# Attention and gated feed-forward in one interleaved kernel: the first sequence's long attention steps turned by VectorE blocks and DMA, as in the other sequences

## The chip, the cores and the metric

The kernel runs on one core of one Trainium2 chip. The time is device microseconds (us) of one execution; a kernel's time is the median of its runs.

## What is computed

Four sequences of 512 rows with 512 columns go through a layer norm, and then through two branches. One is causal attention with 16 heads of 32 columns (normed and rotated queries and keys). The other is a gated feed-forward of 1408 hidden columns whose weights come as integers with a scale. The result is the input plus the product of the branches:

```python
def reference(x, ...):
    xn = _layernorm(x, axis=-1)
    q, k, v = split(xn @ w_qkv)              # 16 heads of 32
    q, k = rotate(rmsnorm(q, q_gamma)), rotate(rmsnorm(k, k_gamma))
    attn = softmax(where(causal, q @ k.T / sqrt(32), -1e30))
    s = (attn @ v) @ w_out
    W = lambda wq, scale: (wq - 128.0) * scale[:, None]
    h = silu(xn @ W(wq_gate, s_gate).T) * (xn @ W(wq_up, s_up).T)
    g = silu(h @ W(wq_down, s_down).T)
    return x + s * g
```

## The kernel before, in words

**Parts.** The work is cut into 16 parts `(b, g)`: sequence `b` of 0 to 3, and group `g` of 0 to 3, which is four heads (one each on 32 of TensorE's rows) and a chunk of the 11 blocks of hidden columns (2 blocks in `g = 0`, 3 in the others). A part has two windows. In the *hidden window* (`hidden_window`) TensorE computes gate and up of the chunk's blocks (`hidden`, L577, 16 matmuls of 512 columns for each block), ScalarE and VectorE form the gated product (L588 to L596), and `fresh.turn` (L416) transposes this part's queries and keys into `qT` and `kT`. In the *attention window* four steps `t` of 128 query rows follow, with 128, 256, 384 and 512 keys: scores on TensorE (L444), the masked minimum on VectorE (L465), the exponential on ScalarE (L475), the transposed probabilities times `v` on TensorE (`values`, L531). Between them stand the chunk's down projection (`contract`, L606, with its addition on VectorE, L617 or L619) and the projection of queries, keys and values for the next part (`product`, L368, and `rotate`, L383 to L406, on ScalarE, VectorE and GpSimd). The order of all of this is written out by hand: every engine takes its instructions in the order in which the code issues them.

**Two ways to turn probabilities.** `Step.turn` (L491, L125, L127) has TensorE transpose 128x128 squares into PSUM, and ScalarE or VectorE copy them to SBUF. `Step.blocks` (L508) has VectorE transpose 32x32 squares within SBUF, one instruction for each head, and `Step.spread` (L522) moves the blocks to their partitions by four DMAs of SyncE's queue (192 KB each for 384 keys, 256 KB each for 512).

**Two orders.** Parts of sequence 0 use `attention_window` (L723): steps 0 to 2 are turned by TensorE there, the four products of the projection are spread over the window, and step 3 is turned by TensorE in the next hidden window (`drain`, L679), at whose end its `values` stand (L721). Parts of sequences 1 to 3 but the very last use `placed_window` (L788): steps 0 and 1 are turned by TensorE with ScalarE's copies, step 2 by `blocks` and `spread`; then come the four products one after the other, then the values of steps 0 to 2, and step 3's scores. Step 3 is turned by `blocks` and `spread` in the next hidden window, and its `values` stand in the next attention window. `swapped(b)` (L419), which is `b > 0`, chooses. The very last part has `last_window`.

**Weights.** The feed-forward's integer weights are prepared in sequence 0 beside the parts, up to the third hidden window, by `weights()` (L278), which is called after each block of a hidden window and after each product of an attention window. One call handles two pieces: it finishes two that were turned at least two calls ago (`finish_weights`, L265, VectorE), starts the loads of two (`load_weights`, L247, SyncE's queue, 256 KB each), and turns two that were loaded in an earlier call (`turn_weights`: a cast on ScalarE, L256, then a DMA transpose on SyncE's queue, L258). A load's room comes free at a finish, so the loads of a call wait for that call's finishes. SyncE's queue issues in order: what waits there holds up all behind it. After the third hidden window `find_wide` (L293 to L297) reduces a flag on VectorE and TensorE.

Of the kernel before, what the change touches and what calls it, by code (L numbers as in the profile page):

```python
# [51 lines left out]
def interleaved(  # L52
# [225 lines left out]
    def weights(n=2):  # L278

        now[0] += 1  # L280
        for _ in range(n):
            if turning and now[0] - turning[0][0] >= 2:
                finish_weights()
        load_weights(n)
        for _ in range(n):
            if loaded and now[0] - loaded[0][0] >= 1:
                turn_weights()
# [11 lines left out]
    units = [(b, g) for b in range(B) for g in range(NC)]  # L299
# [116 lines left out]
                    nc.tensor.transpose(tp[:, ts(t, P)], self.qk[t][:, ts(i, P)], ident)  # L416
                copy(i == 0, dst, tp)

    def swapped(b):  # L419

        return b > 0


    class Step:
        def __init__(self, b, g, t, v, sums, pv):
            self.b, self.g, self.t, self.v, self.sums, self.pv = b, g, t, v, sums, pv
            self.keys = (t + 1) * P
            self.id = f"{b}_{g}_{t}"

            self.per = min(HPG, N // self.keys)  # L430
            self.pieces, self.probs, self.turned = [], [], []
            self.before = None
            self.placed = swapped(b) and (b, g) != units[-1]
            if self.placed:
                self.first, self.way = (8, 9, 0, 0)[t], (None, None, 8, 4)[t]

# [236 lines left out]
    def hidden_window(b, g, last, fresh, result, norm, beside):  # L673

        placed = last is not None and last.placed

        def drain(i):  # L679
            if last is not None and not placed:  # L680
                last.turn(i, scalar=False)
                last.turn(i + 1, scalar=True)

        def turned(*tiles):
            if norm is not None:
                for t in tiles:
                    norm.turn(t)

        fills = [
            lambda: drain(0),  # L690
            lambda: drain(2),
            lambda: (last.spread_sums() if last is not None else None, fresh.turn()),
            lambda: turned(0, 1),
            lambda: turned(2),
            lambda: turned(3),
        ]
        for i, f in enumerate(chunks[g]):
            bank = hidden(b, f, 0, other=placed and i == 0)
            sil = gate(b, f, bank)
            if placed and i == 0:  # L700
                last.blocks(0, 1, 2)
            if fills:
                fills.pop(0)()
            bank = hidden(b, f, 1, other=placed and norm is None and f == chunks[g][-1])
            gated(sil, f, bank, h[:, i])
            if placed and i == 0:
                last.blocks(3)
                last.spread()
            if fills:
                fills.pop(0)()  # L710
            if result is not None:
                result.gate(2 * i)
                result.gate(2 * i + 1)
            for e in beside[i]:
                e()
            if b == 0:
                weights()
        if last is not None:
            last.turn_sums()
            if not placed:  # L720
                last.values()  # L721

    def attention_window(b, g, last, s, fresh, norm):  # L723

        def halves(*tiles):
            if norm is not None:
                for t in tiles:  # L730
                    norm.cut(t)

        def project(t):
            fresh.product(t)

        def rotate(t):
            fresh.rotate(t)

        def beside(t):
            weights()  # L740

        s[0].scores()
        s[1].scores(s[0].whole, s[0].keys)
        s[0].probabilities(0, 1, 2, 3)
        add = contract(b, g, 0)
        s[1].probabilities(0)
        add()
        s[1].probabilities(1, 2, 3)
        if last is not None:
            last.divide()  # L750
        add = contract(b, g, 1, other=True)
        halves(0, 1)
        s[0].turn(0, scalar=False)
        project(0)
        add()
        rotate(0)
        beside(0)
        add = contract(b, g, 2)
        s[0].values()
        s[2].scores()  # L760
        add()
        s[2].probabilities(0, 1, 2, 3)
        s[1].turn(0, scalar=True)
        s[1].turn(1, scalar=False)
        project(1)
        rotate(1)
        halves(2, 3)
        beside(1)
        add = contract(b, g, 3)
        s[1].values()  # L770
        s[3].scores()
        add()
        s[3].probabilities(0, 1)
        s[2].turn(0, scalar=True)
        s[3].probabilities(2)
        s[2].turn(1, scalar=False)
        s[3].probabilities(3)
        project(2)
        s[2].turn(2, scalar=True)
        s[2].turn(3, scalar=False)  # L780
        rotate(2)
        beside(2)
        project(3)
        s[2].values()
        rotate(3)
        beside(3)

    def placed_window(b, g, last, s, fresh, norm, result):  # L788

        def halves(engine, *tiles):
            if norm is not None:
                for t in tiles:
                    norm.cut(t, engine)

        def beside(t):
            if result is not None:
                result.project(t)
                result.finish(t)  # L800

        def load(*tiles):
            if result is not None:
                for t in tiles:
                    result.load(t)

        load(0)
        s[0].scores()
        s[1].scores(s[0].whole, s[0].keys)
        s[0].probabilities(0, 1, 2, 3)  # L810
        add = contract(b, g, 0)
        s[1].probabilities(0, 1, 2, 3)
        add()
        add = contract(b, g, 1, other=True)
        if last.placed:
            last.values()
        s[2].scores()
        add()
        s[2].probabilities(0, 1)
        add = contract(b, g, 2)  # L820
        s[0].turn(0, scalar=True)
        s[2].probabilities(2)
        s[1].turn(0, scalar=True)
        s[2].probabilities(3)
        s[1].turn(1, scalar=True)
        s[2].blocks(0, 1, 2, 3)
        s[2].spread()
        load(1, 2)
        add()
        last.divide()  # L830
        halves(nc.gpsimd, 0, 1)
        for t in range(NT):
            fresh.product(t, other=t == NT - 1)
            fresh.rotate(t)
            if t == 1:
                halves(nc.vector, 2, 3)
            beside(t)
            if t == 1:
                load(3)
        for t in range(3):  # L840
            s[t].values()
        s[3].scores()
        s[3].probabilities(0, 1, 2, 3)
        contract(b, g, 3)()
# [103 lines left out]
    fresh, last, norm, done = prologue(), None, None, None  # L948
    for u, (b, g) in enumerate(units):
        result = Result(b - 1) if g == 0 and b else None  # L950
        done = result or done
        beside = [[], [], []]
        if g == NC - 2 and b + 1 < B:
            for t in range(NT):
                load_x(b + 1, t)
            norm = Norm(b + 1)
            beside[1] += [lambda t=t: norm.stats(t) for t in (0, 1)]
            beside[2] += [lambda t=t: norm.stats(t) for t in (2, 3)]
            beside[2].append(lambda: norm.roots(slice(0, NT)))
        if g == NC - 1 and b + 1 < B:  # L960
            for i, tiles in enumerate(((0, 1), (2, 3))):
                beside[i] += [lambda t=t: norm.apply(t) for t in tiles]
        due = norm if g == NC - 1 and b + 1 < B else None
        hidden_window(b, g, last, fresh, result, due, beside)
        if g == 1 and b:
            for t in range(NT):
                done.store(t)
        if (b, g) == (0, NC - 1):
            nc.sync.dma_start(wout, w_out.rearrange("(c p) m -> p c m", p=P))
        if (b, g) == (0, NC - 2):  # L970
            find_wide()
        s = steps(b, g, fresh.v)
        if u + 1 == len(units):
            break
        fresh = Projection(*units[u + 1])
        if swapped(b):
            placed_window(b, g, last, s, fresh, due, result)
        else:
            attention_window(b, g, last, s, fresh, due)
        last = s[3]  # L980
    result = Result(B - 1)
    for t in range(NT):
# [474 lines left out]
```

## Time and profile before

| | us |
|---|---|
| median of 3 runs (lowest, highest) | 694.18 (692.93, 695.31) |
| the profiled execution's own time | 694.41 |
| its span, first to last instruction | 692.6 |
| TensorE busy in the span | 646.3 (93%) |
| VectorE busy | 442.3 (64%) |
| ScalarE busy | 364.6 (53%) |
| GpSimd busy | 321.3 (46%) |
| mean granted TensorE clock | 0.987 |

A part is told here from its first score matmul to the next part's. Those of sequence 0 start at 41.62, 83.76, 126.37 and 167.35 us from the span's start, those of sequence 1 at 203.19, 252.13, 288.69 and 327.15, and sequence 2 begins at 363.66. The page's lines give, for a group of instructions, the source line, the engine, the operation, the tiles written and read, the shape and the count; then busy time and the mean of one; then the idle time of the engine just before them, and what ended it. A row of the timeline gives start, duration, engine, line and operation, and in brackets the engine's idle time ahead of it with the instruction that ended it.

### The profile page before, as it was taken

Reading aid. Unit: us, or ns where it says so; the run is one execution under the profiler, and the core shown is the slowest. Engines: PE = TensorE matmul, PEld = TensorE weight load, DVE = VectorE, ACT = ScalarE, POOL = GpSimd, SP = SyncE. Lnnn points to the kernel's source line nnn. Section 1 sums busy time; section 2 is a strip of 40 time slices with the busy share of each in tenths; the row PEclk is TensorE's granted clock in tenths of the full one; section 3 lists DMA queues with packets and bytes.
Section 4 is the critical chain, followed back from the end, with each engine's and each line's share of the span. In section 5 each row is a group of like instructions: output and inputs, shape, how many; then the busy total and the mean of one; then the engine's idle time right before and its main releaser. Section 6 shows DMA issues by size and latency. Waiting matters only on the chain.

```text
span 692.6 us, 11843 instructions
## 1 busy us (share of the span) xinstructions
PE 646.3 (93%) x4078; PEld 435.0 (63%) x4078; DVE 442.3 (64%) x1206; ACT 364.6 (53%) x931; POOL 321.3 (46%) x371
## 2 busy tenths in 40 slices
PE   4969999999998999999989999999997999999895
PEld 3645857667674576768665576767665566666652
DVE  3548676755665466867777367788686466757563
ACT  3466666556563264646746055465747146464550
POOL 4905434452754625545462732627281641727322
PEclk9989999999999999999999999999999999999998
DMA  7673744100003044222222134312123304222401
GB/s 245 170 180 102 183 109 103 62 1 1 1 17 92 1 121 108 62 46 63 46 58 55 56 79 113 95 39 38 38 45 77 92 2 121 46 62 47 122 1 66
DMA packets 47408, 51.36 MB, mean 74 GB/s; under 512 B 21206, under 2 KB 31212, under 8 KB 47340
## 3 DMA queue, kind: packets, MB, share of 16 engines
q1 hardware_dynamic: 46380, 50.10, 28.6%
q8 instruction: 34, 0.56, 0.3%
q10 hardware_dynamic: 960, 0.43, 0.2%
q14 instruction: 34, 0.28, 0.1%
HBM read 21.80 MB, written 4.19 MB: 38 GB/s over the span
## 4 chain that ended last, share of the span: by engine, by line
PE 80%; DVE 7%; ACT 6%; DMA 3%; issue 2%; POOL 1%; SPq 1%; DVEq 0%; ACTq 0%
PE qkv L368 24%; PE h L577 21%; PE dn L606 9%; PE so L649 8%; PE pv L531 5%; PE sc L444 5%; PE pt L491 4%; ACT arena L475 2%; PE qkt L416 2%; DVE sil L594 1%; DMA oT<-in_L_ffn_wq_up 1%; POOL h L596 1%; PE xnt L344 1%; ACT arena L125 1%; DVE arena L508 1%
## 5 line engine op out<-in xcount | busy, mean ns | idle before, releaser
L475 ACT ACTIVATE arena<-arena,least 128x128 f32<-128x128 f32 (+3 forms) x256 | 141.2, 553 | 70.8 <-DVE least L465 70.7
L368 PE MATMUL qkv<-wqkv,xnT 128*128 128x384 f32 x512 | 173.3, 491 | 2.3 <-DVE least L465 2.3
L368 PEld LDWEIGHTS qkv<-wqkv,xnT 128*128 128x128 f32 x512 | 96.0, 192 | 66.7 <-issue 5.1
L465 DVE CUSTOM_DVE_ANT_0 arena<-sc,mask 128x128 f32<-128x128 f32 (+3 forms) x256 | 109.9, 487 | 33.8 <-PE sc L444 33.6
L404 POOL TENSOR_TENSOR qk<-qk,qs 128x256 f32<-128x256 f32 x64 | 46.7, 730 | 169.6 <-DVE qs L399 169.6
L596 POOL TENSOR_TENSOR h<-sil,h 128x512 fp32r<-128x512 f32 x44 | 58.3, 1324 | 120.8 <-ACT h L595 120.8
L315 POOL TENSOR_TENSOR ss<-ss,minus_half 128x8 f32<-128x8 f32 x64 | 106.8, 1669 | 5.3
L606 PE MATMUL dn<-wdT,h 128*128 128x512 f32 x352 | 100.3, 421 | 4.9 <-POOL h L596 2.9
L508 DVE STREAM_TRANSPOSE arena<-arena 128x384 f32<-128x384 f32 (+1 forms) x88 | 81.2, 968 | 15.9 <-ACT arena L475 11.1
L606 PEld LDWEIGHTS dn<-wdT,h 128*128 128x128 f32 x352 | 63.2, 191 | 42.5 <-issue 18.4
L383 ACT ACTIVATE squares<-qkv 128x256 f32<-128x256 f32 x64 | 24.7, 385 | 122.2 <-PE qkv L368 103.9
L594 DVE SCALAR_TENSOR_TENSOR sil<-h,scales,sil 128x512 f32<-128x512 f32 x44 | 32.6, 741 | 65.4 <-PE h L577 53.6
L396 DVE TENSOR_TENSOR qk<-qkv,tab 128x256 f32<-128x256 f32 x64 | 27.0, 421 | 72.6 <-ACT v L384 72.1
L595 ACT CAST h<-sil 128x512 fp32r<-128x512 f32 x44 | 27.3, 621 | 76.8 <-DVE sil L594 76.8
L649 PE MATMUL so<-wout,oT 128*128 128x512 f32 x128 | 58.1, 593 | 0.0
L444 PE MATMUL sc<-kT,qT 32*128 32x512 f32 (+3 forms) x512 | 50.8, 478 | 5.9 <-ACT qT L125 5.9
L577 PE MATMUL h<-xh,wuT 128*128 128x512 f32 x176 | 51.0, 412 | 5.2 <-DVE kT L127 5.2
L491 PE MATMUL pt<-ident,arena 128*128 128x128 f32 x332 | 46.7, 276 | 6.5 <-ACT arena L125 6.4
L491 PEld LDWEIGHTS pt<-ident,arena 128*128 128x128 f32 x332 | 38.1, 141 | 22.1 <-ACT arena L125 9.0
L577 PE MATMUL h<-xl,wuT 128*128 128x512 f32 x176 | 49.7, 405 | 0.0
L577 PE MATMUL h<-xh,wgT 128*128 128x512 f32 x176 | 49.3, 402 | 0.0
L577 PE MATMUL h<-xl,wgT 128*128 128x512 f32 x176 | 48.1, 395 | 0.0
(90 smaller groups left out, 916.8 us busy)
## 6 DMA issues: line engine op xcount, KB each, us to landing
arena<-arena SPq DMA_DIRECT2D x44, 256.0 KB, 4.7
arena<-arena SPq DMA_DIRECT2D x44, 192.0 KB, 3.6
x<-in_L_attn_x SPq DMA_DIRECT2D x16, 256.0 KB, 4.6
out<-o SPq DMA_DIRECT2D x15, 256.0 KB, 4.5
xr<-in_L_attn_x SPq DMA_DIRECT2D x12, 256.0 KB, 2.7
wqkv<-in_L_attn_w_qkv SPq DMA_DIRECT2D x4, 576.0 KB, 5.2
wout<-in_L_ffn_wq_up SPq DMA_DIRECT2D x6, 256.0 KB, 3.0
wout<-in_L_ffn_wq_down SPq DMA_DIRECT2D x5, 256.0 KB, 4.0
```

The costliest lines, as they stand in the source:

```text
L315: nc.gpsimd.tensor_tensor(dst, dst, minus_half[:, : dst.shape[-1]], ALU.pow)
L368: nc.tensor.matmul(bank.rearrange("p (i d) -> p i d", i=3), lhsT=xnT[:, c, ts(t, P)], rhs=wqkv[:, c, :, self.g, :], start=(c == 0), stop=( ...
L404: nc.gpsimd.tensor_tensor(qk, qk, qs, ALU.add)
L444: nc.tensor.matmul(bank, lhsT=qT[rows, ts(self.t, P)], rhs=kT[rows, : self.keys], start=True, stop=True,)
L465: nc.vector.tensor_tensor_reduce(out=pr, in0=self.banks[j], in1=mask[:, N - self.keys :], scale=float(HD), scalar=3.0e38, op0=ALU.add, op1 ...
L475: nc.scalar.activation(pr, pr, AF.Exp, bias=least, scale=-1.0, accum_out=self.sums[:, self.t, j : j + 1],)
L491: nc.tensor.transpose(tp[:, ts(i * (self.t + 1) + k, P)], self.probs[n * self.per + i][:, ts(k, P)], ident,)
L508: nc.vector.transpose(piece(self.way, self.t + 1)[:, : HPG * self.keys].rearrange("p (c m k) -> p c m k", c=4, k=32)[:, :, j * n : (j + 1) * n
L577: nc.tensor.matmul(bank, lhsT=w[:, c, ts(f, P)], rhs=a[:, c, :], start=(c == 0 and a is xh), stop=(c == NC - 1 and a is xl),)
L596: nc.gpsimd.tensor_tensor(to[:, 1, :], sil, to[:, 0, :].bitcast(F32), ALU.subtract)
L606: nc.tensor.matmul(bank, lhsT=h[:, i, a, ts(t, P)], rhs=wdT[:, f, :], start=(i == 0 and a == 0), stop=(f == fs[-1] and a == 1),)
L649: nc.tensor.matmul(self.banks[t], lhsT=oT[:, g, ts(t, P)], rhs=wout[:, g, :], start=(g == 0), stop=(g == NC - 1),)
```

## The change

Every part but the last is now `placed`, so sequence 0 takes `placed_window` too; `attention_window`, `drain` and `swapped` are gone. In `placed_window`, `weights()` is called after each of the four products where `b == 0`, and `last.values()` and `last.divide()` are left out in the very first part, which has no predecessor. In a hidden window of sequence 0, step 3's `spread()` is issued behind the first block's `weights()`, not ahead of it. The work of `weights()` is the same, in the same number of calls.

```diff
-    def swapped(b):
-        return b > 0
...
-            self.placed = swapped(b) and (b, g) != units[-1]
+            self.placed = (b, g) != units[-1]
...
-        placed = last is not None and last.placed
-
-        def drain(i):
-            if last is not None and not placed:
-                last.turn(i, scalar=False)
-                last.turn(i + 1, scalar=True)
+        placed = last is not None
...
         fills = [
-            lambda: drain(0),
-            lambda: drain(2),
+            lambda: None,
+            lambda: None,
...
             if placed and i == 0:
                 last.blocks(3)
-                last.spread()
+                if b:
+                    last.spread()
...
             if b == 0:
                 weights()
+                if placed and i == 0:
+                    last.spread()
         if last is not None:
             last.turn_sums()
-            if not placed:
-                last.values()
-
-    def attention_window(b, g, last, s, fresh, norm):
...
     def placed_window(b, g, last, s, fresh, norm, result):
...
         def beside(t):
+            if b == 0:
+                weights()
             if result is not None:
                 result.project(t)
                 result.finish(t)
...
-        if last.placed:
+        if last is not None:
             last.values()
...
-        last.divide()
+        if last is not None:
+            last.divide()
...
-        if swapped(b):
-            placed_window(b, g, last, s, fresh, due, result)
-        else:
-            attention_window(b, g, last, s, fresh, due)
+        placed_window(b, g, last, s, fresh, due, result)
```

## The prediction

> Parts are numbered 4b + g below, so parts 0 to 3 are sequence 0 and part 5 is (1, 1); "stall" is a wait of TensorE.
>
> **What bounds the kernel now.** First the page's busy shares and its chain of work that ended last; then the rows by window for a part of each order; then the timelines of SyncE's queue, ScalarE and TensorE.
>
> ```profile
> PE 646.3 (93%) x4078; PEld 435.0 (63%) x4078; DVE 442.3 (64%) x1206; ACT 364.6 (53%) x931; POOL 321.3 (46%) x371
> ...
> PE 80%; DVE 7%; ACT 6%; DMA 3%; issue 2%; POOL 1%; SPq 1%; DVEq 0%; ACTq 0%
> ```
>
> TensorE is the bound: work taken from it counts, if nothing else comes late. The windows show part 1 (old order) and part 5 (new order), with the same chunk size:
>
> ```profile
> core 0: us, PE busy (x) PEld busy (x) DVE busy (x) ACT busy (x) POOL busy (x), PEclk, DMA share, GB/s
> 83.76:126.37 42.61, 40.35 (x273) 27.97 (x269) 31.51 (x101) 27.22 (x68) 18.56 (x22) 1.00 0.44 107
> 252.13:288.69 36.56, 36.06 (x241) 25.07 (x241) 26.10 (x71) 20.14 (x53) 17.20 (x20) 1.00 0.43 113
> ```
>
> Part 5 is 6 us shorter. But part 1 has more on VectorE and ScalarE: the weights' finishes and casts, which part 5 doesn't have. Their way runs through SyncE's queue, here at the one place where two calls of weights() already stand one product apart:
>
> ```profile
> 67.49 0.33 SPq L247 DMA_DIRECT2D wout<-in_L_ffn_wq_up  x1
> 68.10 0.33 SPq L247 DMA_DIRECT2D wout<-in_L_ffn_wq_gate  x1
> 68.47 2.88 SPq L258 DMA_TRANSPOSE oT<-oT  x2
> 71.45 0.52 SPq L247 DMA_DIRECT2D wout<-in_L_ffn_wq_up  x1
> ```
> ```profile
> 70.05 0.62 ACT L256 CAST wout<-wout 128x512 bf16<-128x512 uint32 x1 [1.32 <-DMA wout<-in_L_ffn_wq_up]
> ```
>
> The load issued at 67.49, as soon as a finish freed its room, is what ScalarE's cast waited for until 70.05: 2.6 us. A spread holds the queue longer (part 5, steps 2 and 3):
>
> ```profile
> 264.90 2.99 SPq L522 DMA_DIRECT2D arena<-arena  x4
> ...
> 282.55 4.14 SPq L522 DMA_DIRECT2D arena<-arena  x4
> ```
>
> **What the Trainium skill says.** "VectorE: DVE Perf Modes", The three transpose paths: VectorE transposes only 32x32 blocks, so moving blocks between partitions is left to something else; the trace agrees, each of the 88 block transposes (968 ns) belongs to a spread. "DMA: Bandwidth & Descriptors", Issuing engines are not separate DMA queues: all DMAs share 16 engines and interleave; here the x loads issued behind part 5's first spread took 4.2 us to land, against 2.6 above. "TensorE: Matmul & The Clock Gate", What's actually happening: an idle window of about 3.4 us halves the clock until it is busy for as long. The trace agrees: after the stall of 2.61 us at 521.3 the granted clock of 522 to 526 is 0.65, of 518 to 522 still 0.92.
>
> **The change part by part.**
>
> *TensorE's transposes.* Steps 2 and 3 lose 12 + 16 transposes in each of parts 0 to 3. Eight take 0.79 us (70.27 to 71.06), so 112 x 0.1 = 11 us. VectorE gets 4 blocks of 0.80 and 4 of 1.03 (7.3 us a part) and loses six copies of about 0.6 (3.6). Its busy 29.7 and 31.5 us in parts 0 and 1 stay below a part's length, so this is free where nothing waits for VectorE.
>
> *The parts, read from the same order elsewhere.* Part 0 becomes part 4 (48.94) without its four output products (3 x 3.43 + 3.53 = 13.8), with ScalarE's table load 0.44 later after the score (1.96 against 1.52): 35.6, against 42.14 now: -6.5. Part 1 becomes part 5 (36.56) with the flag: 1.44 now, and 1.0 more since step 3's values no longer cover the wait: 39.0 against 42.61: -3.6. Part 2 becomes part 6: 38.46 against 40.98: -2.5. Part 3 becomes part 7, with its stall of 2.6 for the copy of kT: 36.51 against 35.84: +0.7. Part 4 becomes part 8, which begins with the values moved out of part 3: 49.87 against 48.94: +0.9. Sum: -11.0. This is without weights beside them.
>
> *weights() in the loop of products.* Four calls now stand 2.6 us apart, the pace of the products. A call holds SyncE's queue for two loads (0.4 each) and two DMA transposes (2.5): 3.3. In part 0 the first product starts at 41.62 + 8.64 + 0.44 = 50.7; step 2's blocks end at about 54.2; its four DMAs end at 57.2, and behind them are queued all weights of this window. The second call's first load goes out at 60.5 and lands at 63.1 (2.6); the third call's cast (0.52) waits for it, behind the cast the fourth product's square and copy (0.43), behind these VectorE's rotation (1.06) and two finishes (1.2): 66.3. Step 3's minima wait there; without weights they start at 50.7 + 13.0 = 63.7 (part 5: 274.68 - 261.66). So 2.6 late. TensorE feels it at two banks: the first up product needs the first minimum's bank (66.9 against 66.5: 0.4), and the keys' transposes the first gate's, held until exponentials, table load and silu are done (71.7 against 71.0: 0.7). +1.1, so part 1's scores come at 78.3.
>
> *The spread behind weights(), and a load behind the spread.* From 66.3: minima 2.45, addition 0.6, three blocks 3.05, gated product 0.7, fourth block 1.05, first finish 0.6: 74.8. Then SyncE's queue: two loads 0.95, two transposes 2.5, the spread 4.15: 82.4. Only then goes the next call's first load, landing at 85.0; the hidden window's last cast waits for it (both are in program order; no wait can be skipped), and behind that cast on ScalarE are the copy of the sums, the table load and all exponentials of part 1. From that copy to the first product part 5 takes 261.66 - 253.18 = 8.5, 0.4 of it a wait for VectorE that will be over: 85.0 + 0.5 + 8.1 = 93.6. Part 5's pace gives 78.3 + 9.5 = 87.8: +5.8. The spread's own landing (82.4 + 4.7 = 87) stalls step 3's values too, but is covered by this longer wait. Bounds: 4.2 if the load shares the DMA engines with the spread as the x loads did (+1.6), and 2.6 less if the loop comes without lag. I take 2.6, measured for this very kind of load.
>
> *Part 1's loop.* The same lag; its down products are 0.5 longer, so only the second bank counts: +0.7. In its hidden window all loads are over, but four finishes precede the flag's reduction on VectorE: about 1 of the lag reaches TensorE (estimate; 0 to 2.6): +0.9. During that stall ScalarE gets ahead, and the small waits at a part's start (0.27 and 0.24 in part 5) go: -0.5. Parts 2 and 3 have no weights; their casts and DMAs cost nothing.
>
> *Sum:* -11.0 + 1.1 + 5.8 + 0.7 + 0.9 - 0.5 = -3.0. Against the profiled execution: 694.41 - 3.0 = 691.4; it is 0.2 above the median, so 691.2 for the median.
>
> **The rivals.** *The cover holds.* The loads land in time everywhere, and only the two last casts (1.05) come late at a part's start, with some 0.5 at the banks: -11.0 + 1.5 = -9.5, 684.7. For it: DMA share is only 0.56 and 0.44 in parts 0 and 1, VectorE and ScalarE have 10 us spare. Against it: 3.3 us of queue for each 2.6 us product, and the order of load behind spread. *Slower: the load behind the spread lands late and TensorE's clock drops.* At the start of part 1 TensorE waits for the spread's landing, then for exponentials; at the flag about 3 us more. If the late load takes 4.2 (+1.6), loads in both loops lengthen likewise (+1.0), and each of the two stalls brings one half-clock stretch of 3.4 us (1.7 lost, as after 359.9): -3.0 + 1.6 + 1.0 + 3.4 = +3.0, 697.2. It decides once these together cost over 3.0: a landing of 5.6 alone would do, or both half-clock stretches.
>
> **How the numbers follow.** A difference of 0.3% (2.1 us) is about what a measurement of this kernel can tell from none. Forecast (1 to 6 us won) 0.40, of which 0.28 is a win over 2.1; cover 0.27; slower rival 0.33, of which 0.04 stays within 2.1. Faster 0.55, same 0.16, slower 0.29. The likeliest case alone spans 688 to 693; the range goes to 685.0 (cover, short of its end) and 697.5 (the slower rival with its costs in full).
>
> **What would show it.** In the profile after: part 1's scores near 78, its first product near 94, and ahead of it ScalarE idle several us at a cast that waits for a load; SyncE's queue with spread and load back to back near 78 to 83; step 3's minima some 2.6 late in parts 0 and 1 but not in part 2, which should take 38; part 4's scores some 4 us ahead of 203.19 (the last +0.9 comes after them). A part 0 to 1 boundary without a ScalarE wait for a DMA would make the cover rival right; a granted clock near 0.5 at part 1's and part 2's starts the slower one.

## The result, and the profile after

| | before | after |
|---|---|---|
| median of 14 runs each, us (lowest, highest) | 695.17 (692.75, 696.55) | 697.56 (695.92, 700.82) |
| ratio, 95% interval | | 1.0044 (1.0028 to 1.0060) |
| the profiled execution's own time, us | 694.41 | 695.95 |
| its span, us | 692.6 | 694.1 |

The change makes the kernel slower: by 0.44% by the ratio of the runs, by 0.34% by the two medians. The forecast was 691.2 with 685.0 to 697.5 as its range; the sign is wrong, and the median lies 0.06 above the range. The rival nearest to it is the "slower" one, at 697.2.

TensorE's line and the chain of work that ended last, from the page of the kernel after:

```profile
PE 633.9 (91%) x3966; PEld 424.4 (61%) x3966; DVE 456.1 (66%) x1216; ACT 360.8 (52%) x923; POOL 318.1 (46%) x369
...
PE 72%; DVE 8%; DMA 7%; ACT 6%; issue 3%; SPq 1%; POOL 1%; DVEq 0%; ACTq 0%
```

The 112 transposes are gone (4078 matmuls to 3966), and 12.4 us of busy TensorE with them (646.3 to 633.9). Yet the span is 1.5 longer: TensorE's share of the chain fell from 80% to 72%, and DMA's rose from 3% to 7%. Where this is lost shows in the windows of parts 0 to 3 of the kernel after (columns as before):

```profile
core 0: us, PE busy (x) PEld busy (x) DVE busy (x) ACT busy (x) POOL busy (x), PEclk, DMA share, GB/s
41.49:81.71 40.22, 36.77 (x201) 25.38 (x201) 31.78 (x94) 26.56 (x66) 17.27 (x20) 0.91 0.66 142
81.71:130.87 49.16, 40.23 (x242) 27.20 (x241) 35.78 (x104) 26.93 (x66) 18.61 (x22) 0.93 0.69 153
130.87:170.14 39.27, 39.03 (x257) 27.69 (x256) 27.38 (x72) 19.58 (x54) 17.17 (x21) 0.96 0.25 57
170.14:205.43 35.29, 32.43 (x226) 22.19 (x225) 26.62 (x70) 22.49 (x58) 18.79 (x21) 1.00 0.26 65
```

Part 0 won 1.9 us (42.14 before), part 1 lost 6.6 (42.61), part 2 won 1.7 and part 3 0.6. In part 1 TensorE has 9 us without work, and its granted clock is 0.93. At part 5's start the kernel is 3.6 us behind the one before.

The way into the loss is the one that the prediction drew. SyncE's queue in part 0's loop of products, and at the end of its hidden window:

```profile
53.83 3.21 SPq L518 DMA_DIRECT2D arena<-arena  x4
57.12 1.03 SPq L247 DMA_DIRECT2D oT<-in_L_ffn_wq_down  x2
58.25 2.62 SPq L258 DMA_TRANSPOSE wout<-wout  x2
...
62.48 1.19 SPq L258 DMA_TRANSPOSE wout<-wout  x1
63.78 1.23 SPq L258 DMA_TRANSPOSE oT<-oT  x1
65.10 1.37 SPq L247 DMA_DIRECT2D wout<-in_L_ffn_wq_up  x1
...
80.77 4.20 SPq L518 DMA_DIRECT2D arena<-arena  x4
85.07 0.54 SPq L247 DMA_DIRECT2D wout<-in_L_ffn_wq_up  x1
```

ScalarE's casts wait for these loads, and VectorE's finish for the transpose (the bracket: idle time ahead, and what ended it):

```profile
60.94 0.62 ACT L256 CAST oT<-oT 128x512 bf16<-128x512 uint32 x1 [3.89 <-DMA oT<-in_L_ffn_wq_down]
...
69.19 0.62 ACT L256 CAST wout<-wout 128x512 bf16<-128x512 uint32 x1 [3.78 <-DMA wout<-in_L_ffn_wq_up]
...
89.21 0.62 ACT L256 CAST wout<-wout 128x512 bf16<-128x512 uint32 x1 [5.76 <-DMA wout<-in_L_ffn_wq_up]
```
```profile
67.62 0.69 DVE L265 TENSOR_SCALAR_CACHE_REDUCE wdT<-wout 128x512 fp32r<-128x512 bf16 x1 [1.55 <-DMA wout<-wout]
...
68.84 0.69 DVE L461 CUSTOM_DVE_ANT_0 arena<-sc,mask 128x512 f32<-128x512 f32 x1
```

From issue to the cast that it releases, the loads of 57.12, 65.10 and 85.07 took 3.8, 4.1 and 4.1 us, not 2.6. The DMA transpose issued at 62.48 took 5.1, and the finish that waits for it stands ahead of step 3's minima on VectorE. They begin at 68.84, not at the 66.3 of the prediction. TensorE in turn (part 0, then part 1's start, then part 1's hidden window):

```profile
69.59 2.08 PE L573 MATMUL h<-xh,wuT 128*128 128x512 f32 x4 [2.50 <-DVE least L461]
...
88.56 1.08 PE L527 MATMUL pv<-arena,v 128*32 128x128 f32 x32 [2.32 <-DMA arena<-arena]
...
96.95 0.66 PE L487 MATMUL pt<-ident,arena 128*128 128x128 f32 x4 [2.20 <-ACT arena L125]
97.45 5.00 PE L368 MATMUL qkv<-wqkv,xnT 128*128 128x384 f32 x15
...
115.97 1.38 PE L573 MATMUL h<-xh,wuT 128*128 128x512 f32 x4 [1.86 <-DVE least L461]
```

The four matmuls behind the stall of 2.50 take 2.08 us; elsewhere four take 1.10. The clock is halved there. Two windows of the kernel after show it:

```profile
69.50:73.00 3.50, 3.41 (x9) 2.77 (x10) 3.50 (x11) 3.48 (x10) 0.21 (x1) 0.58 0.79 206
90.00:94.00 4.00, 4.00 (x20) 2.44 (x16) 2.00 (x8) 3.97 (x13) 0.00 (x0) 0.64 0.80 194
```

There are four such stretches of 3.4 us in parts 0 to 2, from 69.0, 89.5, 116.8 and 130.5, each at or right behind a stall of 1.9 to 2.5; a stretch costs up to 1.7 of TensorE's work, half its length. The kernel before has none from 47 to 361 us; both end a longer one at part 0's start (at 45.1 and 46.9). Over its 14 runs the median granted clock of the kernel after is 0.980. That of the kernel before, over the runs beside the experiments, is 0.987.

### The profile page after: what moved, and what is told of

It reads as the page before. It is cut to its first block, busy times and chain, and to the rows that moved or that the text cites. A ratio compares the mean times of both kernels' runs of the same rounds, so it can differ in the third digit from the quotient of the medians.

```text
span 694.1 us, 11735 instructions
## 1 busy us (share of the span) xinstructions
PE 633.9 (91%) x3966; PEld 424.4 (61%) x3966; DVE 456.1 (66%) x1216; ACT 360.8 (52%) x923; POOL 318.1 (46%) x369
## 4 chain that ended last, share of the span: by engine, by line
PE 72%; DVE 8%; DMA 7%; ACT 6%; issue 3%; SPq 1%; POOL 1%; DVEq 0%; ACTq 0%
PE qkv L368 21%; PE h L573 20%; PE dn L602 9%; PE so L645 8%; PE pv L527 5%; PE sc L440 4%; PE pt L487 3%; ACT arena L471 3%; DVE arena L504 2%; DMA arena<-arena 2%; DVE sil L590 2%; PE qkt L416 2%; DMA oT<-in_L_ffn_wq_up 1%; ACT arena L125 1%; DMA oT<-oT 1%
## 5 line engine op out<-in xcount | busy, mean ns | idle before, releaser
L368 PE MATMUL qkv<-wqkv,xnT 128*128 128x384 f32 x512 | 169.9, 487 | 0.0
L504 DVE STREAM_TRANSPOSE arena<-arena 128x384 f32<-128x384 f32 (+1 forms) x120 | 110.6, 971 | 23.6 <-ACT arena L471 16.2
L591 ACT CAST h<-sil 128x512 fp32r<-128x512 f32 x44 | 27.3, 620 | 70.8 <-DVE sil L590 70.8
L471 ACT ACTIVATION_READ_ACCUMULATOR arena<-arena,least 128x1 f32 x256 | 48.0, 187 | 0.0
L527 PE MATMUL pv<-arena,v 128*32 128x128 f32 x1280 | 42.0, 275 | 4.0 <-DMA arena<-arena 4.0
```

The source lines that it names most:

```text
L368: nc.tensor.matmul(bank.rearrange("p (i d) -> p i d", i=3), lhsT=xnT[:, c, ts(t, P)], rhs=wqkv[:, c, :, self.g, :], start=(c == 0), stop=( ...
L471: nc.scalar.activation(pr, pr, AF.Exp, bias=least, scale=-1.0, accum_out=self.sums[:, self.t, j : j + 1],)
L504: nc.vector.transpose(piece(self.way, self.t + 1)[:, : HPG * self.keys].rearrange("p (c m k) -> p c m k", c=4, k=32)[:, :, j * n : (j + 1) * n
L527: nc.tensor.matmul(self.pv[j * HD : (j + 1) * HD, ts(self.t, P)], lhsT=self.v[:, k, ts(j, HD)], rhs=self.turned[j][:, k], start=(k == 0), ...
```

## The experiments

The lengths of parts are those of each profiled execution, which can lie some us off the median of its kernel's runs (e6 2.1 above it, e8 3.6 and e12 2.6 below). The kernel before ran beside each group: medians 693.75 (e1 to e4), 694.14 (e5 to e8), 694.10 (e9, e10) and 694.12 (e11, e12).

| | time | ratio to before (95%) | part 0 | part 1 | part 2 |
|---|---|---|---|---|---|
| before | 694 to 695 | | 42.14 | 42.61 | 40.98 |
| the change | 697.56 | 1.0044 (1.0028 to 1.0060) | 40.22 | 49.16 | 39.27 |
| e1 only parts 2, 3 | 690.5 | 0.9947 (0.9926 to 0.9969) | 42.57 | 42.60 | 36.91 |
| e2 spread by GpSimd | 702.75 | 1.0130 (1.0096 to 1.0164) | 41.86 | 50.39 | 40.70 |
| e5 no later loads | 688.11 | 0.9916 (0.9892 to 0.9939) | 37.78 | 42.60 | 39.43 |
| e6 no later DMA transposes | 692.24 | 0.9979 (0.9967 to 0.9992) | 37.84 | 45.89 | 39.47 |
| e7 four more rooms | 694.33 | 0.9996 (0.9977 to 1.0015) | 40.80 | 43.45 | 40.61 |
| e8 spread first | 698.31 | 1.0076 (1.0048 to 1.0103) | 40.80 | 48.89 | 37.92 |
| e9 calls spaced | 696.70 | 1.0033 (1.0021 to 1.0045) | 38.67 | 48.94 | 39.45 |
| e10 spaced and rooms | 688.76 | 0.9913 (0.9890 to 0.9935) | 37.38 | 42.86 | 39.47 |
| e11 and the flag moved | 684.78 | 0.9870 (0.9846 to 0.9894) | 36.97 | 38.97 | 39.70 |
| e12 neither loads nor transposes | 683.95 | 0.9853 (0.9829 to 0.9878) | 35.82 | 39.27 | 37.93 |

The theory: the new order itself is worth what was forecast, and loads and DMA transposes of the weights that land late take it away, each wait being passed down the in-order queues to TensorE. Rivals: VectorE, which got the blocks, has become the bound; or the queue's order alone (a load behind the spread) costs it; or the added bytes do.

**e1: the new order in parts 2 and 3 only**, which have no loads.

```diff
-    def swapped(b):
-        return b > 0
+    def swapped(b, g):
+        return (b, g) >= (0, 2)
```

> Only parts 2 and 3 of sequence 0, which have no weights beside them, take the new order; parts 0 and 1 keep the old one. Late-loads theory: the loss of the change lies in parts 0 and 1 alone, so this one wins what parts 2 and 3 win: part 2 becomes 38.5 us instead of 41.0, parts 3 and 4 stay within 0.5 of before, with no weights' DMA, ScalarE cast or half clock at part 2's start: 691 to 693, ratio to before 0.994 to 0.998. VectorE theory (the 7.3 us of block transposes in each part are the loss, weights or not): no gain or a loss, 695 to 697.

It is 0.53% faster than before. Part 2 takes 36.91 (part 1 leaves it no values), part 3 35.28, part 4 50.27: against 40.98, 35.84 and 48.94 that is 3.3 us won, which is the whole difference. VectorE gets its blocks there too, so they are not what costs.

**e2: sequence 0's spreads issued by GpSimd.**

```diff
-                nc.sync.dma_start(
+                (nc.sync if self.b else nc.gpsimd).dma_start(
```

> As the change, but in sequence 0 the spreads are issued by GpSimd's queue, so that no load or transpose of the weights stands behind a spread on SyncE's queue. If the order of issue on SyncE's queue is the cause: the load that part 1's first casts wait for goes out about 4 us earlier, the loop's first load 3 us earlier, 692 to 694. If the 16 DMA engines, which all of these share, are the cause: the loads still take 4 us to land, and it gains under 2 us: 695.5 to 698. Worse than 698 if the issue on GpSimd delays the rotations.

Slower still: the third case of the expectation. The rotation on GpSimd does begin later behind the spread's issue (at 57.33 in part 0, in the change at 55.25). With the spread out of SyncE's queue, ScalarE's casts wait as before. The waits from 41 to 131 us of this kernel (total, times, longest):

```profile
ACT wout L256 <- DMA wout<-in_L_ffn_wq_up: 9.3, 2, 6.4
ACT oT L256 <- DMA oT<-in_L_ffn_wq_down: 8.1, 3, 4.9
```

In the change they are 9.5 and 7.0. Spread and weights now go out side by side and share the DMA engines: the median DMA of step 3's spread lands after 5.8 us here and 4.2 in the change. The Trainium skill says ("DMA: Bandwidth & Descriptors", Issuing engines are not separate DMA queues) that DMAs of all issuing engines run on the same 16 DMA engines and interleave; that the loads land no sooner here agrees with it. SyncE's queue, with no spread of its own in it, now stands in two DMA transposes:

```profile
79.40 0.33 SPq L247 DMA_DIRECT2D oT<-in_L_ffn_wq_gate  x1
79.78 7.06 SPq L258 DMA_TRANSPOSE wout<-wout  x2
86.94 0.57 SPq L247 DMA_DIRECT2D wout<-in_L_ffn_wq_up  x1
```

Two take 2.5 in the change. The next load goes out at 86.94, later than the 85.07 of the change. Why these transposes hold the queue was not tried, nor how much of the rest is GpSimd's own: its DMAs also stand under another kind in the trace's list of queues (software_dynamic), so this run moves more than the place of issue.

**e3 and e4: the change, and the kernel before, without weights' DMAs** after the first eleven loads and eight DMA transposes. Casts and finishes stay.

```diff
-                nc.sync.dma_start(raw.bitcast(U32), src.bitcast(U32))
+                if n_prep - len(todo) <= 11:
+                    nc.sync.dma_start(raw.bitcast(U32), src.bitcast(U32))
...
-        nc.sync.dma_start(turned, halves_[:, :n], transpose=True)
+        if len(turning) + len(finished) < 8:
+            nc.sync.dma_start(turned, halves_[:, :n], transpose=True)
```

> As the change, but after the first 11 loads and 8 DMA transposes of weights no further one is issued; the casts and finishes stay and work on what lies in their rooms, so the feed-forward's weights are not the reference's. Late-loads theory: with the DMA waits gone, the new order reaches nearly what the same order gives in sequence 1: 684 to 687. VectorE theory (finishes and block transposes together are too much beside the products): the loop's lag stays, 694 or more. In between, 688 to 692, if half of the lag is engine work.

> The kernel before with the same loads and transposes of weights left out (weights not the reference's). Control for the run above. Late-loads theory: the old order hides these DMAs nearly wholly (two waits of 1.3 and 1.4 us of ScalarE, neither on TensorE's path), so 691 to 694.5, that is at most 3 us less than before. If it falls by more than 6 us, the old order paid for these DMAs as well, and the theory of what the new order adds is wrong.

The left-over contents set the flag for large weights, and the float32 fallback ran behind the kernel (1879.74 and 1892.99 us in all), so only the first parts can be read. Without weights' DMAs the old order hardly changes: parts 0 and 1 take 41.96 and 42.59. The new one falls from 40.22 and 49.16 to 35.66 and 39.27. So the loss is an effect of these DMAs on the new order. The finishes, casts and blocks are all still there, so VectorE as the bound is out.

**e12: the same cut in the change, with the flag held off** (`EXACT_MAX = 1.0e30`), for a time that can be read.

> The changed kernel without loads after the first eleven and without DMA transposes after the first eight (the weights are wrong), casts and finishes kept, and the flag held off, so that its own time can be read. If the forecast's minus 11.0 for the parts without weights is right, and the weights' DMAs are all that took it away: part 0 near 35.7, part 1 near 39.3, and 681 to 685 in all. If the minus 11.0 itself is wrong by the half-clock stretches or the rest: 686 to 690.

683.95 us, 10.2 below the kernel before in the same comparison (8.5 to 11.9 by the interval), as expected. The forecast's "-11.0", "without weights beside them", holds.

**e5 and e6: only the loads, or only the DMA transposes, left out** (one half each of the edit above, and the flag held off).

> The changed kernel without the loads of integer weights after the first eleven; casts, DMA transposes and finishes all stay (on left-over contents, so the weights are wrong), and the flag is held off. Theory A, late loads: ScalarE's casts waiting for loads that land after about 4 us, and all behind them, is most of the loss: part 0 near 37, part 1 near 42 (40.2 and 49.2 with the loads), 686 to 688. Theory B, late DMA transposes: the finishes that wait for transposes are most of it: part 1 stays above 46, 693 to 696. Rival, VectorE's extra work: 696 to 698, no change.

> The changed kernel without the DMA transposes of weights after the first eight; loads, casts and finishes all stay (the weights are wrong), and the flag is held off. Theory A, late loads: part of the loss stays, since a load still goes out behind a finish and a spread, but it lands sooner with fewer bytes beside it: part 1 near 43, 687 to 690. Theory B, late transposes: part 0 near 36, part 1 near 40, 682 to 685. Rival, VectorE's extra work: 696 to 698.

Each alone frees 2.4 us of part 0, both together 4.4. In part 1 the loads are worth 6.6 and the transposes 3.3; both together 9.9. By the ratios of whole runs it is 8.9 and 4.5 us, and 13.3 together, so the two shares about add up. e5 came 0.1 above what was expected of late loads. e6 is above what either theory said: with the transposes gone, casts still wait up to 3.8 us for a load. Loads are the larger share, but neither alone is the cause.

**e8: the one placement undone**, the spread ahead of `weights()`.

```diff
-                if b:
-                    last.spread()
+                last.spread()
...
-                if placed and i == 0:
-                    last.spread()
```

> The changed kernel with step 3's spread issued ahead of the first block's weights() in sequence 0, as in the other sequences: the one placement of the change undone. My prediction charged 5.8 us to the order of a load behind the spread. If that order is the cost, the spread lands earlier, and with it part 1 gets about 4 shorter: 692 to 694. If it is that loads and spread share the queue and the DMA engines whichever goes first (the same call's loads are then behind the spread, and the next cast waits for those), it stays within 2 of the change: 696 to 699.

No gain: 698.31, part 1 at 48.89. Now that call's own loads stand behind the spread, and a cast waits for them (SyncE's queue, then ScalarE, in this kernel):

```profile
76.98 4.17 SPq L518 DMA_DIRECT2D arena<-arena  x4
81.25 0.55 SPq L247 DMA_DIRECT2D oT<-in_L_ffn_wq_up  x1
```
```profile
85.59 0.62 ACT L256 CAST oT<-oT 128x512 bf16<-128x512 uint32 x1 [4.91 <-DMA oT<-in_L_ffn_wq_up]
```

The load behind the spread takes 4.3 us from issue to cast here and 4.1 in the change, whichever call it belongs to. So the order of the two alone is not the cause. What stays is that the next cast needs the load at once; the next runs change that.

**e9: the four calls spaced apart**, 5 to 7 us instead of 2.6.

```diff
-            if b == 0:
+            if b == 0 and t % 2:
                 weights()
...
+        if b == 0:
+            weights()
         for t in range(NT):
...
         s[3].probabilities(0, 1, 2, 3)
+        if b == 0:
+            weights()
```

> The changed kernel with all its work; only the places of the four calls of weights() in sequence 0's attention windows change: ahead of the first product, after the second, after the fourth and after step 3's probabilities, 5 to 7 us apart instead of 2.6. Late-landing theory: a landing of 4 to 5 us fits between such calls, so part 0 is 37 to 38 (40.2 in the change); the load behind step 3's spread is left as it is, so part 1 still waits at its start, but has no lag from its loop: 44 to 47 (49.2). Total 688 to 693. Rival, the bytes themselves (the sum of the DMAs' traffic is what slows, wherever the calls stand): within 2 of the change, 696 to 699.

Part 0 gains 1.5 us; part 1 gains nothing, and the total is 0.9 below the change, which is not clear of noise (the intervals overlap). I missed the total: I had taken part 1's loss to lie in its loop as much as at its start. The wait at its start, with two half-clock stretches behind it, keeps part 1 at 48.94:

```profile
88.56 0.62 ACT L256 CAST wout<-wout 128x512 bf16<-128x512 uint32 x1 [6.12 <-DMA wout<-in_L_ffn_wq_up]
```

**e7: four more rooms, and one call more between load and cast.** The x tiles, idle in parts 0 and 1, take loads, so a load no longer waits for a finish of its own call.

```diff
+        spare.extend(xp.tile([P, D], F32, tag="x", name=f"spare_{i}") for i in range(4))
+        rooms.extend(spare)
...
-            if loaded and now[0] - loaded[0][0] >= 1:
+            if loaded and now[0] - loaded[0][0] >= (2 if now[0] < 12 else 1):
...
-        if len(finished) >= NC:
+        if len(finished) >= NC and not (now[0] > 9 and any(room is s for s in spare)):
             rooms.append(room)
```

> The changed kernel with all its work. The four tiles that hold x before and after sequence 0's first parts serve as four more rooms for loads until part 1, so that a load does not wait for a finish of its own call, and a cast takes a piece that was loaded two calls ago, not one. If lateness of loads is the cause, the loss goes: part 0 near 37, part 1 near 41, part 2 near 39, 683 to 687, faster than both. If it is the bytes and queue time themselves (3.3 us of SyncE's queue for each 2.6 us product), the loop still lags and it is 692 to 696. VectorE theory: 696 to 698.

Part 1 gains 5.7 us, part 0 nothing, and the total is 694.33, 7 above what late loads as the cause were to give and within the 692 to 696 of the rival (bytes and queue time). The casts' wait has become a wait of the finishes for their transposes, and TensorE stalls longer behind it than in the change. The waits of this kernel from 41 to 82 us:

```profile
DVE wuT L266 <- DMA spare<-spare: 5.2, 2, 3.3
```
```profile
PE h L574 <- DVE least L462: 3.3, 1, 3.3
```

**e10: both mends together.**

> Both mends together: the calls spaced as in the run before it, and the four more rooms with one call more between load and cast. Late-landing theory: no cast and hardly any finish waits for a DMA in parts 0 and 1: part 0 near 37, part 1 near 41, and few half-clock stretches: 681 to 686, the fastest of all. Rival, the bytes themselves: 691 to 696.

688.76, 2.8 above the theory's range and 2.2 below the rival's. Together the mends are worth more (1.3% from the change's ratio to its own) than e7 (0.5%) and e9 (0.1%) added up. A likely reason, not tried apart, is that either mend alone leaves a stall: e9 that of part 1's start, e7 that of the finishes. Part 1 ended in a wait of TensorE for the flag:

```profile
121.83 0.27 PE L296 MATMUL largest_t<-ident,largest_row 128*1 128x128 f32 x1 [3.72 <-DVE largest_row L294]
```

**e11: and the flag's transpose behind part 2's attention window** (`find_wide` returns its row; `tell_wide`, with the rest of it, stands behind `placed_window`).

> The run with both mends, and the flag's transpose on TensorE (3.7 us of wait at part 2's start there, with a half-clock stretch behind it) moved behind part 2's attention window; VectorE's reduction stays where it was. If the wait is a true stall of TensorE: part 2's products come 1.2 to 3.7 earlier, and one half-clock stretch (up to 1.7) goes: 684 to 687, against 688.8. If VectorE is what part 2's start waits for (its minima follow the same finishes), only the first 1.2: 687 to 688.5.

684.78, as expected, and the fastest version with all work in it: 1.3% below the kernel before, and within 1 us of e12, which has no weights' DMAs after the first ones. Not all of the 1.3% need be the new order's: neither the mends nor the flag's move was tried in the kernel before, where the flag costs TensorE 1.44 at part 2's start. Its windows of parts 0 and 1:

```profile
41.51:78.48 36.97, 36.04 (x200) 24.49 (x200) 31.25 (x91) 25.85 (x65) 17.06 (x20) 0.93 0.76 152
78.48:117.45 38.97, 36.59 (x241) 25.38 (x241) 32.97 (x95) 25.75 (x65) 17.32 (x21) 1.00 0.78 173
```

The DMA share is higher than in the change (0.76 and 0.78 against 0.66 and 0.69), and single DMAs are not clearly faster: the median load into `wout` for the up weights takes 4.0 us here, 3.8 there, the median DMA of step 3's spread 4.8 and 4.2. So the bytes are not the cause. What differs is how soon after the issue somebody waits. TensorE has some 1 and 2 us without work in these parts instead of 3 and 9, and from 47 to 190 us no half-clock stretch is left.

## Why the prediction was wrong

| | predicted | measured |
|---|---|---|
| the parts without weights' DMAs | -11.0 | -10.2 (e12) |
| part 0's first product | 50.7 | 50.59 |
| part 0's length | 36.7 | 40.22 |
| in it, start of step 3's minima | 66.3 | 68.84 |
| part 1, from its scores to its first product | 15.3 | 15.74 |
| part 1, the rest | 31.1 | 33.42 |
| part 2 (with the -0.5 behind the flag's stall) | 38.0 | 39.27 |
| part 3 | 36.5 | 35.29 |
| part 4 | 49.9 | 50.27 |

**What held.** The reading from the same order elsewhere; the view that TensorE's transposes leave the path and that VectorE's blocks are free; the order of SyncE's queue; and the place at part 1's start. The predicted picture, a ScalarE idle several us at a cast ahead of part 1's exponentials, is there. Its length was right within 0.5, in part by luck: the load took 4.1 us, 1.5 more than charged, but it went out only 2.7 late where part 1's scores were 3.4 late, and from its landing to the first product it was 0.4 less.

**What failed** is the step "weights() in the loop of products", by its size and by what it let land in time. It priced one path at 66.3: the second call's load, a cast, the rotation, two finishes, the minima. That load went out at 60.99, not 60.5, and landed after 2.85 us, near the 2.6 that the step took; the rotation behind it ends about 1.0 late. What the step put at nothing is the DMA transposes that the two finishes wait for. The one that decides was issued at 62.48, behind a spread, four loads and two transposes on SyncE's queue, and took 5.1 us; the finish waits 1.55 for it. So the minima are 5.2 late against the ideal 63.6 (50.59 + 13.0), not 2.6, and TensorE's two small waits of 1.1 together became one stall of 2.50. In part 1's loop the first load behind the spread takes 3.7 us and the two transposes that its last finishes wait for 4.2 and 4.1; the stall is 1.86, not 0.7. The prediction had the longer landing as the bound of another term and did not carry it into the loop.

**What was left out** is the clock. The likeliest case valued half-clock stretches at nothing, though it quoted one of the trace before; the slower rival had two. Four came. Part 0's excess of 3.5 is the longer stall (1.4 more than charged) and one stretch (TensorE works through 2.8 us of it, so about 1.4); some 0.7 stay open. Part 2's 1.3 is the stretch behind the flag: in e8 and e12, which have none there, part 2 takes 37.92 and 37.93, as forecast. How the 2.3 of part 1's rest divide into its stall, the flag (2.46 with its transpose, where 3.3 was charged) and two stretches was not measured apart. The clock also hides in part 3, where the forecast was too high: its 36.5 was read from part 7 of the kernel before, which holds most of the stretch at 361. In the trace after, parts 3, 7 and 11 all take 35.3. The stretches at 361 and 521 did not occur there, which won 1.2 in part 7 and 1.6 in part 11. No step foresaw that, and it is most of why 3.6 us behind at part 5 became 1.5 at the end. It was chance (see the last section). That profiled execution is also 1.6 below the median of the change's runs.

**The rivals.** The slower one came by its mechanism: late loads, stalls, and half-clock stretches at part 1's and part 2's starts. That its number is so near (697.2 against 697.56; +3.0 against the +2.4 of the medians) is in part luck, since the longer landing did not lengthen part 1's start and four stretches came in parts 0 to 2, not two. It should have been the likeliest: its bound of 4.2 was the one measured beside a spread. The cover failed at both places that it named.

## What to carry to other kernels

Price a transfer's landing from a place where the same neighbours run, not from its quietest row; where calls hand work to the next call, ask how much later than that row it may land before the chain slips, for in a chain of in-order queues the lateness adds up. The cure here was not fewer bytes or another queue but distance: room to start a load one call earlier, and consumers further apart. The two together were worth more than each by itself added up. And a stall of TensorE of about 2 us may be charged nearly twice, once for itself and once for the clock behind it, or only once, by where it falls; so a part's length read from a trace may hold a stretch that the next execution doesn't have.

## What the runs showed of the hardware

- Whether a stall halves the clock depends on where it falls. The Trainium skill ("TensorE: Matmul & The Clock Gate", What's actually happening) lets the clock fall after an idle window of about 3.4 us; it also calls that window free-running. The trace agrees with the grid: the four stretches of the trace after last 3.41 us each and start 20.5, 27.3 and 13.7 us apart, which is 6, 8 and 4 times 3.41. It does not agree with a window that is idle throughout, and the stall of 2.61 that the prediction took for agreement doesn't either. In the windows of this grid just ahead of the four stretches TensorE is idle for 1.93, 2.32, 1.86 and 2.05 us. The stall of 2.20 at 96.95 is cut by the grid into 1.6 and 0.6, and no stretch follows. The clearest pair is the wait for the copy of `kT` in part 7, before and after, with the windows of each trace's grid (columns as above):

```profile
359.94 1.23 PE L577 MATMUL h<-xh,wuT 128*128 128x512 f32 x4 [2.61 <-DVE kT L127]
...
357.55:360.96 3.41, 1.02 (x4) 0.86 (x5) 2.33 (x4) 2.29 (x4) 1.09 (x2) 1.00 0.76 111
360.96:364.37 3.41, 3.41 (x21) 2.57 (x23) 1.39 (x3) 0.60 (x2) 0.00 (x0) 0.50 0.66 199
```
```profile
363.48 1.20 PE L573 MATMUL h<-xh,wuT 128*128 128x512 f32 x4 [2.62 <-DVE kT L127]
...
359.16:362.57 3.41, 1.70 (x12) 1.27 (x10) 3.41 (x4) 1.04 (x2) 1.27 (x1) 1.00 0.19 22
362.57:365.98 3.41, 2.50 (x13) 1.92 (x13) 1.12 (x4) 1.86 (x4) 0.61 (x1) 1.00 0.92 203
```

  The same stall halves the clock where 2.39 us of it lie in one window, and doesn't where 1.71 is the most. Sorted in this way, the traces of all kernels but e3 and e4 put the limit near 1.8 us idle, about half a window: a stretch follows from 1.75 on, and none up to 1.90 at the most, with one exception (0.96, in e6). Where the grid lies in the span differs from trace to trace.
- A load of 256 KB that took 2.6 us in the kernel before took 3.7 to 4.3 right behind a spread, and a DMA transpose issued some us behind one up to 5.1. With the spread on GpSimd's queue (e2) the median load into `oT` for the down weights took 5.8, so in that run landings came later, not earlier.
- VectorE's 32 block transposes more (120 at a mean of 971 ns) added 13.8 us to its busy time net of the copies that went, and the time hardly shows it: e12, with all of them, comes to -10.2 where -11.0 was forecast with the blocks free.
